# Layer 0 of a two-layer cross-attention kernel: norms placed behind the turned keys' factor, last maxima of the argmax quarters two places later, weights loaded by ScalarE's queue

## The chip, the cores and the metric

The kernel runs on one core of a Trainium2 chip. A core has five engines, each of which runs its own list of instructions in order: TensorE (PE in the profile, with its weight loads as PEld), VectorE (DVE), ScalarE (ACT), GpSimd (POOL) and SyncE (SP), which here only issues DMAs. They wait for each other through semaphores. SBUF is the on-chip memory of 128 partitions; TensorE writes its products to the banks of PSUM, from which VectorE or ScalarE fetch them. The metric is device time in microseconds, the median of several executions. The kernel before takes 1864.41 us (median of 3 runs, 1863.96 to 1866.86).

## What is computed

32 sequences of 64 tokens of width 512 pass through two layers, each a cross-attention and a feed-forward part, always added to x. The change touches layer 0's attention and the choice that prepares its feed-forward part. Cut to these:

```python
x = x + L0_xattn(layernorm(x), ctx)
def L0_xattn(text, features):
    features_n = rmsnorm(features, fn_w)
    Q = rmsnorm(text @ Wq.T + bq, qn_w)
    K = rmsnorm(features_n @ Wk.T + bk, kn_w)
    attn = softmax(Q @ K.T * D ** -0.5)
    return attn @ features_n
x = x + L0_ffn(layernorm(x))
def L0_ffn(x):
    inter = x @ c1_w.T @ c2_w.T               # 1792 wide
    idx = argmax of each block of 32 in inter # 56 choices a token
    h = relu(w1[idx] . x);  return sum of h * w2t[idx]
...                                           # layer 1: 32-head attention, clustered feed-forward
```

All of it is float32.

## The kernel before

**Tiles and pairs.** The 2048 tokens are 16 tiles of 128 rows, worked on as NP = 8 pairs of two tiles (index tt or u). Layer 0's attention is one loop over i from 0 to 7, at whose step i pair i is projected and the scores of pair i - 1 and the values of pair i - 2 are done. This text calls step i "iteration i".

**The chain of one pair.** `norm(i)` takes the tokens' mean and variance (`ln_stats`, L104 and L105), the root of the variance on ScalarE (L330), a reciprocal (L331) and then writes the normed tokens `xn` (`ln_apply`, L108, two instructions). `norm_context` squares and sums the context on ScalarE (L341), takes the root (L342) and a reciprocal (L343): `rs`, the context's factor. `keys_of` turns `xn` (transposes on TensorE at the helper's line L181, a copy on ScalarE at L365), multiplies the turned context `ct` with WK (`pk`, L372), and evacuates with factor and bias to `kb` (L375). `queries_of` multiplies the turned tokens with WQ (`pq`, L392), adds the bias (`qb`, L393), and turns that (`ptq`, copied by L400). In the next iteration `turn_keys` multiplies `kb` with its norm (L410), turns it (`ptk`) and writes the turned keys times a column of weights, `kT` (L415, two instructions). `scores` multiplies queries and `kT` (`psc`, L427), takes the maximum (L432), scales it (L434), takes exponentials on ScalarE (L440), and writes the weighted context, `cn` times `rs` times `fnb`, in place (L446, two instructions), which the values need. An iteration later `turn_scores` (L454, L456) and `add_values` (`po`, L466) make the values, and L472 adds them to x.

**The argmax.** A tile has four quarters of 448 columns (14 blocks of 32). `two_quarters(p, v)` computes two of them for pair p (`pi`, L277, into PSUM), and `first_largest` takes block maxima (`m`, L267), compares (`e`, L268, `is_equal`), lets GpSimd multiply `e` with a falling ramp (L272), and hands back a function for the last instruction, the maximum of that product (`choice`, L273). These functions wait in the list `begun`; `choose_begun` empties it at the start of the next `two_quarters`. The table PLAN says at which iteration and which of three places (0 to 2) these steps stand: `two_quarters` for pair 0 at (4,1), (4,2), (5,0), (5,1), for pair 1 at (6,0), (6,1), (7,0) and once behind the loop; `turn_choice`, which empties the list too, at (5,2).

**What sets the order.** The kernel's text gives a program order; a scheduler builds each engine's list from it, the earlier instruction of the program first, but one that it reckons ready sooner may overtake. `tc.issue_after(ins)` places what its block adds behind `ins` in the list of the same engine (an order, no wait). `started_behind(normed)` makes GpSimd's weight sums of an iteration (for w2, and eight of w1 in iterations 3 to 7, L127) wait until the weighted context of that iteration is written.

**Buffers.** The products `pk`, `pq`, `po` and `pi` share three PSUM banks (`ps_m`, tag `pm`), taken in turn. `e0`, the tile of `e`, has two buffers, the default of its pool; `xn` two, `cn` four.

**Loads.** SyncE issues all DMAs. At the start: four parts of the first context `ct` with four parts of WK between them, the tokens of pair 0, four parts of WQ, the context of pair 0, two biases, the tokens of pair 1, and so on (L476 to L488). WK is multiplied by a column on VectorE (L491) before its first use.

Of the kernel before, what the change touches and what calls it, by code (L numbers as in the profile page):

```python
# [8 lines left out]
F32 = mybir.dt.float32  # L9
# [3 lines left out]
ALU = mybir.AluOpType  # L13
# [3 lines left out]
P = 128  # L17
# [3 lines left out]
C = D // P  # L21
NT = B * S // P
INTER = 1792
QW = 448
# [11 lines left out]
def tile_kernel(  # L36
# [25 lines left out]
    nc = tc.nc  # L62
# [39 lines left out]
    def ln_stats(mv, t):  # L102
        st = small.tile([P, 6], F32, name="st", tag="st")
        nc.vector.bn_stats(st, X[t])  # L104
        nc.vector.bn_aggr(mv, st)  # L105

    def ln_apply(xn, t, mean, rstd):
        nc.vector.tensor_scalar(xn, X[t], mean, rstd, ALU.subtract, ALU.mult)  # L108
# [75 lines left out]
    with ExitStack() as l0:  # L184
# [106 lines left out]
        with ExitStack() as pa:  # L291
            wpool = pa.enter_context(tc.tile_pool(name="l0w", bufs=1))
            wk = pa.enter_context(tc.tile_pool(name="l0work", bufs=2))
# [32 lines left out]
            def norm_tokens(i, rs):  # L326
                mv = small.tile([P, 2, 2], F32, name="mv2", tag="mv2")
                for tt in range(2):
                    ln_stats(mv[:, tt, :], 2 * i + tt)
                nc.scalar.activation(rs, mv[:, :, 1], AF.Sqrt, bias=eps5)  # L330
                nc.vector.reciprocal(rs, rs)  # L331
                xn = wk.tile([P, 2, D], F32, name="xn", tag="xn")
                for tt in range(2):
                    ln_apply(xn[:, tt, :], 2 * i + tt, mv[:, tt, 0:1], rs[:, tt : tt + 1])
                return xn

            def norm_context(cn, rs):
                ss = small.tile([P, 2], F32, name="ss", tag="ss")
                for tt in range(2):
                    scr = wk.tile([P, D], F32, name="scr", tag="scr", bufs=1)  # L340
                    nc.scalar.activation(scr, cn[:, tt, :], AF.Square, accum_out=ss[:, tt : tt + 1])  # L341
                nc.scalar.activation(rs, ss, AF.Sqrt, bias=eps6, scale=1.0 / D)  # L342
                nc.vector.reciprocal(rs, rs)  # L343

            def norm(i, cn):

                rs = small.tile([P, 4], F32, name="rs4", tag="rs4")
                xn = norm_tokens(i, rs[:, 0:2])
                if i > 0:
                    norm_context(cn, rs[:, 2:4])  # L350
                return xn, rs

            def norm_of(sq):
                nc.scalar.activation(sq, sq, AF.Sqrt, bias=eps6, scale=1.0 / D)
# [52 lines left out]
            def turn_keys(kb, sq):  # L407
                kT = [wk.tile([P, C, P], F32, name="kT", tag="kT") for _ in range(2)]
                for tt in range(2):
                    nc.vector.tensor_scalar(  # L410
                        kb[:, tt, :], kb[:, tt, :], sq[:, 2 + tt : 3 + tt], None, ALU.mult
                    )
                    pt = ps_t.tile([P, C, P], F32, name="ptk", tag="pt")
                    transposed(pt, kb[:, tt, :])
                    nc.vector.tensor_mul(kT[tt], pt, wqk[:, :, None].to_broadcast([P, C, P]))  # L415
                return kT

            def scores(cn, rs, qT, sq, kT, one=None):


                psc = ps_s.tile([P, 2, S], F32, name="psc", tag="psc")
                for u in range(2):
                    for c in range(C):
                        for h in (1, 0):
                            half = slice(h * S, (h + 1) * S)
                            with tc.high_priority(offset=100) if u or c or not h else ExitStack():
                                product = nc.tensor.matmul(  # L427
                                    psc[half, u, :], qT[:, u, c, half], kT[h][:, c, u * S : (u + 1) * S],
                                    start=c == 0, stop=c == C - 1, skip_group_check=True,
                                )  # L430
                nm = small.tile([P, 2], F32, name="nm", tag="nm")
                nc.vector.tensor_reduce(nm, psc, AX.X, ALU.max, negate=True)  # L432
                if one is None:
                    most = nc.vector.tensor_mul(nm, nm, sq[:, 0:2])  # L434
                else:
                    most = nc.vector.scalar_tensor_tensor(nm, nm, one, sq[:, 0:2], ALU.mult, ALU.mult)
                s1 = wk.tile([P, 2, S], F32, name="s1", tag="s1")
                sm = small.tile([P, 2], F32, name="sm", tag="sm")
                for u in range(2):
                    nc.scalar.activation(  # L440
                        s1[:, u, :], psc[:, u, :], AF.Exp,
                        bias=nm[:, u : u + 1], scale=sq[:, u : u + 1], accum_out=sm[:, u : u + 1],
                    )

                for tt in range(2):
                    normed = nc.vector.scalar_tensor_tensor(  # L446
                        cn[:, tt, :], cn[:, tt, :], rs[:, 2 + tt : 3 + tt], fnb, ALU.mult, ALU.mult
                    )
                nc.vector.reciprocal(sm, sm)
                return s1, sm, (product.ins, most.ins, normed.ins)  # L450

# [23 lines left out]
            for c in range(C):  # L475
                nc.sync.dma_start(ct[0][:, c, :], cT[0][:, c, 0 : 2 * P])  # L476
                if c == 0:
                    nc.sync.dma_start(colt, cols)
                nc.sync.dma_start(WK[:, c, :], wk0[:, c, :])
            load_tokens(0)  # L480
            for c in range(C):
                nc.sync.dma_start(WQ[:, c, :], wq0[:, c, :])
            cn = {0: load_context(0)}
            nc.sync.dma_start(bk, bk0.to_broadcast([P, D]))
            nc.sync.dma_start(bq, bq0.to_broadcast([P, D]))
# [35 lines left out]


            steps = [prep_steps(p, ps_t) for p in range(2)]
            choices, made, begun = {}, {}, []

            def step(p, k):
                made[p] = steps[p][k]()

            def choose_begun():
                while begun:  # L530
                    begun.pop(0)()

            def two_quarters(p, v):
                choose_begun()
                if v == 0:
                    choices[p] = new_choices()
                two = []
                for q in (2 * v, 2 * v + 1):
                    pi = ps_m.tile([P, 1, D], F32, name="pi0", tag="pm")[:, :, 0:QW]

                    with tc.high_priority(offset=100) if two else ExitStack():
                        key_product(pi[:, 0], made[p][1], q // 4, q % 4)
                    two.append((q, pi))
                for q, pi in two:
                    e = wk.tile([P, QW], F32, name="e0", tag="e0")
                    c = choices[p][q // 4][:, NBQ * (q % 4) : NBQ * (q % 4) + NBQ]
                    begun.append(first_largest(pi, e, c, 1))

# [25 lines left out]
            NP = NT // 2  # L574
            store = None
            ready = norm(0, cn[0])
            keys, scored, last = {}, {}, []

            def turn_and_add(i):
# [4 lines left out]
            for i in range(NP):  # L584
# [22 lines left out]
                now = ready  # L607
                if 0 < i < NP - 1:
                    ready = norm(i + 1, cn[i + 1])
                place(i, 0)  # L610
                xn, rs = now
                kb, sq, xT = keys_of(i, ct.pop(i), xn, rs)
                if i == 0:
                    ready = norm(1, cn[1])
                if i:
                    rs1, kb1, sq1, qT = keys.pop(i - 1)
                    add = turn_and_add(i - 2) if i > 1 else lambda: None
                    kT = turn_keys(kb1, sq1)
                    add()
                    *scored[i - 1], (_, _, normed) = scores(cn[i - 1], rs1, qT, sq1, kT)  # L620
                    with started_behind(normed):
                        sum_up()
                        for n in range(*{3: (0, 2), 4: (2, 4), 5: (4, 6), 6: (6, 7), 7: (7, 8)}.get(i, (0, 0))):
                            w = [t[:, :, QW * (n // 4) : QW * (n // 4) + QW] for t in W1]
                            four_sums(nc.gpsimd, w[4:], *w[:4], False, (n % 4,))
# [18 lines left out]
            xT, choices = made[1][0], choices[1]  # L644
# [4 lines left out]
        with ExitStack() as pb:  # L649
            wk = pb.enter_context(tc.tile_pool(name="ffnwork", bufs=2, reuse_waits="tile"))  # L650
# [131 lines left out]
            for p in range(NP):  # L782
# [18 lines left out]
                if choosing:  # L801
                    choices = new_choices()
# [28 lines left out]
    with ExitStack() as pc:  # L831
# [3 lines left out]
        wk = pc.enter_context(tc.tile_pool(name="l1work", bufs=2, reuse_waits="tile"))  # L835
# [303 lines left out]
        kT = keys(kvs[0])  # L1139
        qT, qsq = project_q(xts, 0, 0)  # L1140
        last = None
        for n, (T, g) in enumerate(units):
# [21 lines left out]
            if more:  # L1164
# [5 lines left out]
                kT = keys(kvs[g2 % 2])  # L1170
# [159 lines left out]
```

## Time and profile before

| what | value |
|---|---|
| median of 3 runs | 1864.41 us (1866.86, 1863.96, 1864.41) |
| profiled execution, its own time | 1866.38 us |
| its span in the profile | 1864.6 us, 29382 instructions |
| mean granted clock of TensorE | 0.992 of full speed |
| DMA | 204.58 MB, 110 GB/s on the mean, on one hardware queue beside two of the instructions |
| layer 0's attention | from 0 to about 188 us, then `ph` (L720) of its feed-forward part begins |
| busy from 100 to 120 us | PE 18.84, DVE 14.38, ACT 9.38, POOL 12.50 us |
| busy from 120 to 140 us | PE 17.39, DVE 14.66, ACT 9.23, POOL 8.34 us, granted clock 0.83 |

A line of the profile names engine, line of the kernel, operation and tiles (out <- in). A list in order of time starts with the start and the length in us (of xN instructions together) and ends, in brackets, with the idle time of the engine before it and what ended that. A row of a table by stretches gives the stretch, its length, the busy time of PE, PEld, DVE, ACT and POOL with the number of instructions, then the granted clock of TensorE, the mean busy share of the 16 DMA engines and GB/s. The ends of TensorE's products are modelled, so that a busy PE is not one at its peak.

### The profile page before, as it was taken

How to read it: one execution, taken by the hardware profiler on the slowest of the kernel's cores; microseconds unless marked ns; L12 is line 12 of the kernel's file. 1: busy time of each engine (PE TensorE's matmuls, PEld its weight loads, DVE VectorE, ACT ScalarE, POOL GpSimd, SP SyncE). 2: the span in 40 equal slices, each digit the busy share in tenths (PEclk: the TensorE clock that was granted, in tenths of full speed). 3: DMA queues.
4: the chain of work that ended last, by engine and by line, in shares of the span. 5: the costliest groups of instructions: out<-in, count | busy, mean ns of one | idle time of the engine just before them, and what ended most of it. 6: DMA issues, size and time to landing. Idle time of an engine off the chain costs nothing.

```text
span 1864.6 us, 29382 instructions
## 1 busy us (share of the span) xinstructions
PE 1825.8 (98%) x11612; PEld 1468.1 (79%) x11612; DVE 940.8 (50%) x1715; ACT 652.1 (35%) x1183; POOL 718.8 (39%) x622
## 2 busy tenths in 40 slices
PE   8999999999999999999999999999999999999997
PEld 4544988888998888878888888888888888888753
DVE  5877555555425444345543444444434544444566
ACT  4644322222113333334333333333334333333470
POOL 1542444444336676564322343323224333242300
PEclk9999999999999999999999999999999999999998
DMA  8631400000024444444444354444443444443203
GB/s 242 184 114 53 160 22 21 21 22 21 21 68 151 131 131 149 149 163 135 142 130 131 108 151 122 118 130 119 130 145 116 119 130 119 130 119 96 80 1 90
DMA packets 153592, 204.58 MB, mean 110 GB/s; under 512 B 14512, under 2 KB 95152, under 8 KB 152816
## 3 DMA queue, kind: packets, MB, share of 16 engines
q1 hardware_dynamic: 153456, 202.72, 36.4%
q8 instruction: 92, 1.51, 0.3%
q14 instruction: 44, 0.36, 0.1%
HBM read 173.60 MB, written 29.07 MB: 109 GB/s over the span
## 4 chain that ended last, share of the span: by engine, by line
PE 85%; DVE 4%; POOL 4%; DMA 3%; ACT 3%; issue 2%; SPq 0%; POOLq 0%; ACTq 0%
PE b L893 45%; PE ph L720 10%; PE po L763 9%; PE sc L1046 3%; PE pv L1098 3%; PE pd L1231 3%; POOL prob L1053 2%; PE pr L1015 2%; PE pq L392 2%; PE pta L1083 2%; DVE x L1126 1%; PE pt L181 1%; PE pk L372 1%; DMA x<-in_x 1%; PE pi L277 1%
## 5 line engine op out<-in xcount | busy, mean ns | idle before, releaser
L893 PE MATMUL b<-tx,wq 128*128 128x256 f32 x1024 | 242.8, 381 | 0.5 <-ACT keep L901 0.5
L893 PE MATMUL b<-wo,so 128*128 128x256 f32 x1024 | 233.7, 381 | 3.9 <-DVE x L1126 2.0
L893 PEld LDWEIGHTS b<-wo,so 128*128 128x128 f32 x1024 | 193.0, 190 | 36.1 <-DVE x L1126 9.8
L893 PEld LDWEIGHTS b<-tx,wq 128*128 128x128 f32 x1024 | 191.3, 190 | 31.2 <-issue 6.0
L127 POOL TENSOR_TENSOR so<-oT 128x512 f32<-128x512 f32 x64 | 80.1, 1274 | 338.8 <-ACT oT L1104 338.6
L1126 DVE TENSOR_TENSOR x<-x,b 128x512 f32<-128x512 f32 x224 | 153.4, 685 | 93.3 <-PE b L893 91.7
L893 PE MATMUL b<-wo,oT 128*128 128x256 f32 x768 | 190.0, 383 | 0.0
L893 PE MATMUL b<-xt,wq 128*128 128x256 f32 x768 | 186.9, 381 | 0.0
L901 ACT COPY keep<-b 128x512 f32<-128x512 f32 x144 | 84.1, 585 | 266.1 <-PE b L893 266.1
L893 PEld LDWEIGHTS b<-wo,oT 128*128 128x128 f32 x768 | 143.0, 190 | 20.1
L893 PEld LDWEIGHTS b<-xt,wq 128*128 128x128 f32 x768 | 141.8, 190 | 21.1 <-issue 4.0
L1053 POOL TENSOR_TENSOR prob<-prob,msk 128x512 f32<-128x512 f32 x64 | 80.1, 1273 | 198.8 <-DVE prob L1052 198.8
L982 DVE TENSOR_TENSOR qT<-b,keep 128x512 f32<-128x512 f32 x96 | 66.3, 691 | 129.1 <-PE b L893 129.1
L984 ACT ACTIVATE qsq<-qT 128x512 f32<-128x512 f32 x128 | 80.9, 632 | 116.4 <-DVE qT L982 115.4
L893 PE MATMUL b<-wkv,sc 128*128 128x256 f32 x512 | 115.7, 379 | 0.0
L272 POOL TENSOR_TENSOR e<-e,down 128x896 f32<-128x896 f32 (+1 forms) x40 | 68.3, 1713 | 102.3 <-DVE e L268 92.5
L893 PEld LDWEIGHTS b<-wkv,sc 128*128 128x128 f32 x512 | 97.3, 190 | 13.2
L763 PE MATMUL po<-w,gT 128*128 128x256 f32 x448 | 101.9, 382 | 0.0
L763 PEld LDWEIGHTS po<-w,gT 128*128 128x128 f32 x448 | 84.0, 190 | 18.7 <-issue 7.8
L1061 ACT ACTIVATE prob<-prob 128x512 f32<-128x512 f32 x64 | 40.5, 632 | 150.5 <-POOL prob L1058 150.5
L953 DVE TENSOR_TENSOR kv<-b,keep 128x512 f32<-128x512 f32 x48 | 33.2, 691 | 116.5 <-PE b L893 116.5
L893 PE MATMUL b<-wkv,ct 128*128 128x256 f32 x384 | 91.4, 379 | 0.0
(197 smaller groups left out, 3133.2 us busy)
## 6 DMA issues: line engine op xcount, KB each, us to landing
wq<-in_wq SPq DMA_DIRECT2D x104, 256.0 KB
wo<-in_wo SPq DMA_DIRECT2D x104, 256.0 KB
wq<-wqs SPq DMA_DIRECT2D x96, 256.0 KB
wo<-wos SPq DMA_DIRECT2D x96, 256.0 KB
wkv<-in_wkv SPq DMA_DIRECT2D x52, 256.0 KB
wkv<-wks SPq DMA_DIRECT2D x48, 256.0 KB
wqs<-wq SPq DMA_DIRECT2D x32, 256.0 KB
wos<-wo SPq DMA_DIRECT2D x32, 256.0 KB
```

Of the source, the lines that this page charges most:

```text
L127: ins = eng.tensor_tensor(s[k], *pairs[k], op)
L272: nc.gpsimd.tensor_tensor(e3, e3, down[:, None, :].to_broadcast([P, k, BLK]), ALU.mult)
L720: nc.tensor.matmul(ps[:, c, :], W1[LEFT[i]][:, d, (c0 + c) * P : (c0 + c + 1) * P], xq[RIGHT[i]][:, d, :], start=first and c == 0 and d == ...
L763: nc.tensor.matmul(ps, chunk(gq[LEFT[i]], c), W2[RIGHT[i]][:, c, :], start=first and c == 0, stop=c == HC - 1, skip_group_check=True,)
L893: last = nc.tensor.matmul(out[:, h, :], lhs(h, c), rhs(h, c), start=first and h == 0 and c == 0, stop=c == 1, skip_group_check=True,)
L901: nc.scalar.copy(e, ps)
L982: nc.vector.tensor_add(o, ps, kept.rearrange("p j (b t) -> p j b t", t=S))
L984: nc.scalar.activation(qsq[:, 4 * th : 4 * th + 4, 2 * hh : 2 * hh + 2, :], o, AF.Square)
L1046: nc.tensor.matmul(sc[k * S : (k + 1) * S, 4 * a + 2 * pp + b, :], qT[:, at, 2 * pp + k, :], kT[:, bb * S : (bb + 1) * S], start=True, sto ...
L1053: nc.gpsimd.tensor_tensor(pr, pr, msk_b, ALU.add)
L1098: one = nc.tensor.matmul(pv[b][:, a, :], kv[rows, 2 * h + a, HD : 2 * HD], aTs[h][rows, a, :], start=True, stop=True,).ins
L1126: added.append(nc.vector.tensor_add(xq[:, i, j], xq[:, i, j], ps).ins)
```

## The change

Four things, in the order of the diff. `norm_tokens` no longer writes `xn` itself but hands back `apply`, which does. The call before the loop and iteration 0 run it at once, as before; iterations 1 to 6 run it after `add()`, inside `issue_after(kT_done[-1])`, where `kT_done` is a new list of the last `kT` instruction of each `turn_keys`. The two instructions of the weighted context in `scores` are put into such a block as well. `two_quarters` leaves the last two entries of `begun` in the list, and `e0` has four buffers. The four loads each of WK and WQ are issued by ScalarE.

```diff
                 xn = wk.tile([P, 2, D], F32, name="xn", tag="xn")
-                for tt in range(2):
-                    ln_apply(xn[:, tt, :], 2 * i + tt, mv[:, tt, 0:1], rs[:, tt : tt + 1])
-                return xn
+
+                def apply():
+                    for tt in range(2):
+                        ln_apply(xn[:, tt, :], 2 * i + tt, mv[:, tt, 0:1], rs[:, tt : tt + 1])
+
+                return xn, apply
...
-                    nc.vector.tensor_mul(kT[tt], pt, wqk[:, :, None].to_broadcast([P, C, P]))
+                    done = nc.vector.tensor_mul(kT[tt], pt, wqk[:, :, None].to_broadcast([P, C, P]))
+                kT_done.append(done.ins)
                 return kT
...
                 for tt in range(2):
-                    normed = nc.vector.scalar_tensor_tensor(
-                        cn[:, tt, :], cn[:, tt, :], rs[:, 2 + tt : 3 + tt], fnb, ALU.mult, ALU.mult
-                    )
+                    with tc.issue_after(kT_done[-1]):
+                        normed = nc.vector.scalar_tensor_tensor(
+                            cn[:, tt, :], cn[:, tt, :], rs[:, 2 + tt : 3 + tt], fnb, ALU.mult, ALU.mult
+                        )
...
-                nc.sync.dma_start(WK[:, c, :], wk0[:, c, :])
+                nc.scalar.dma_start(WK[:, c, :], wk0[:, c, :])
             load_tokens(0)
             for c in range(C):
-                nc.sync.dma_start(WQ[:, c, :], wq0[:, c, :])
+                nc.scalar.dma_start(WQ[:, c, :], wq0[:, c, :])
...
-            def choose_begun():
-                while begun:
+            def choose_begun(left=0):
+                while len(begun) > left:
                     begun.pop(0)()

             def two_quarters(p, v):
-                choose_begun()
+                choose_begun(2)
...
-                    e = wk.tile([P, QW], F32, name="e0", tag="e0")
+                    e = wk.tile([P, QW], F32, name="e0", tag="e0", bufs=4)
...
                     kT = turn_keys(kb1, sq1)
                     add()
+
+                    if i < NP - 1:
+                        with tc.issue_after(kT_done[-1]):
+                            ready[2]()
                     *scored[i - 1], (_, _, normed) = scores(cn[i - 1], rs1, qT, sq1, kT)
```

More of the change, by code (lines that the diff above doesn't have):

```diff
@@ L347, in norm @@
                 rs = small.tile([P, 4], F32, name="rs4", tag="rs4")
-                xn = norm_tokens(i, rs[:, 0:2])
+                xn, apply = norm_tokens(i, rs[:, 0:2])
                 if i > 0:
                     norm_context(cn, rs[:, 2:4])
-                return xn, rs
+                return xn, rs, apply
             def norm_of(sq):
@@ L523, in tile_kernel @@
             steps = [prep_steps(p, ps_t) for p in range(2)]
-            choices, made, begun = {}, {}, []
+            choices, made, begun, kT_done = {}, {}, [], []
             def step(p, k):
                 made[p] = steps[p][k]()
-            def choose_begun():
-                while begun:
+            def choose_begun(left=0):
+                while len(begun) > left:
                     begun.pop(0)()
             def two_quarters(p, v):
-                choose_begun()
+                choose_begun(2)
                 if v == 0:
@@ L610, in tile_kernel @@
                 place(i, 0)
-                xn, rs = now
+                xn, rs, _ = now
                 kb, sq, xT = keys_of(i, ct.pop(i), xn, rs)
@@ L614, in tile_kernel @@
                     ready = norm(1, cn[1])
+                    ready[2]()
                 if i:
@@ L619, in tile_kernel @@
                     add()
+                    if i < NP - 1:
+                        with tc.issue_after(kT_done[-1]):
+                            ready[2]()
                     *scored[i - 1], (_, _, normed) = scores(cn[i - 1], rs1, qT, sq1, kT)
```

## The prediction

> **What bounds the kernel now.** I read the page first. TensorE (PE) is busy 98% of the span, so a microsecond counts only if PE stands still in it or runs at a lower clock.
>
> ```profile
> PE 1825.8 (98%) x11612; PEld 1468.1 (79%) x11612; DVE 940.8 (50%) x1715; ACT 652.1 (35%) x1183; POOL 718.8 (39%) x622
> ```
>
> The change touches layer 0's attention only, 0 to about 188 us. Next I asked whom PE waits for in the first 300 us:
>
> ```profile
> PE pk L372 <- DVE WK L491: 5.5, 1, 5.5
> PE psc L427 <- DVE kT L415: 3.3, 3, 2.1
> PE pk L372 <- DVE e L268: 1.2, 1, 1.2
> ```
>
> The columns are total, times, longest. One wait of 2.1 us, of the scores for the turned keys kT, and one of 1.2 us, of the keys' product for an argmax comparison e (`is_equal`), stand out behind the head's 5.5 us. Both lie in iteration 5. The granted clock was read by stretches of 2 us there (third figure from the end):
>
> ```profile
> 120.00:122.00 2.00, 1.01 (x8) 0.13 (x8) 2.00 (x4) 0.05 (x1) 0.73 (x1) 1.00 0.79 242
> 122.00:124.00 2.00, 0.89 (x16) 0.89 (x18) 2.00 (x4) 0.68 (x2) 1.35 (x1) 0.78 0.71 133
> 124.00:126.00 2.00, 2.00 (x26) 1.40 (x22) 1.24 (x4) 0.00 (x0) 0.00 (x0) 0.50 0.96 344
> 126.00:128.00 2.00, 2.00 (x7) 1.01 (x4) 1.17 (x5) 1.83 (x4) 0.00 (x0) 0.50 0.20 68
> 128.00:130.00 2.00, 2.00 (x4) 0.83 (x3) 1.29 (x5) 1.89 (x4) 1.26 (x2) 0.52 0.46 103
> 130.00:132.00 2.00, 2.00 (x6) 0.88 (x5) 1.52 (x3) 0.00 (x0) 1.43 (x2) 1.00 0.41 159
> ```
>
> PE idles, then runs at half clock: 2.0 us x (0.22 + 0.50 + 0.50 + 0.48) = 3.4 us lost. VectorE's (DVE) list in order of time tells why PE idled:
>
> ```profile
> 117.68 0.62 DVE L273 TENSOR_REDUCE choice<-e 128x14 f32<-128x448 f32 x1 [0.50 <-POOL e L272]
> 118.22 0.74 DVE L375 SCALAR_TENSOR_TENSOR kb<-pk,rs,bk 128x512 f32<-128x512 f32 x1
> 118.88 1.00 DVE L108 TENSOR_SCALAR xn<-x,mv,rs 128x512 f32<-128x512 f32 x2
> 119.79 1.41 DVE L446 SCALAR_TENSOR_TENSOR cn<-cn,rs,fnb 128x512 f32<-128x512 f32 x2
> 121.11 0.75 DVE L375 SCALAR_TENSOR_TENSOR kb<-pk,rs,bk 128x512 f32<-128x512 f32 x1
> 121.77 1.28 DVE L415 TENSOR_TENSOR kT<-ptk,wqk 128x512 f32<-128x512 f32 x2
> ```
>
> Four norm instructions (2.4 us) and last maxima that wait for GpSimd (POOL) stand before kT, and DVE runs its list in order.
>
> **Layer norm and context weighting behind kT.** Nothing is added or removed: two `xn` (about 0.5 us each), two `cn` (0.72) per pair move from before kT to after it; no DMA moves. In iteration 5 the keys' last product ends about 118.9, so without the four, kb could end near 119.7 and kT, 1.28 us behind it, near 121.0, just when PE ends the values before the scores; iterations 3, 4, 6 and 7, where kT follows kb directly, have no wait of the scores at all. So the 2.10 us go. In iteration 2 a `cn` pair slowed to 2.84 us by POOL holds kb back, and the scores wait 0.52: 0.5 us go. In iteration 1 the scores wait 0.64 and a transpose 0.40; but kT there also stands behind the context factor's reciprocal (L343, at 36.10), which waits for ScalarE and the context's DMA at 34.26 and is not moved. Between 0 (the DMA holds it) and 1.0 I take 0.6.
>
> What it costs is behind kT. A product in the argmax needs one of three PSUM banks, and the second query product gets the bank of the first argmax quarter, once e has read it. In iteration 6:
>
> ```profile
> 148.63 1.41 DVE L472 SCALAR_TENSOR_TENSOR x<-po,sm,x 128x512 f32<-128x512 f32 x2
> 150.81 1.15 DVE L267 TENSOR_REDUCE m<-pi 128x14 f32<-128x448 f32 x2
> 151.88 1.15 DVE L268 TENSOR_TENSOR e<-pi,m 128x448 f32<-128x448 f32 x2
> ...
> 150.65 7.13 PE L392 MATMUL pq<-WQ,xT 128*128 128x512 f32 x16
> ```
>
> kT ends at 148.57; e is done with the first quarter at 152.5 (3.9 us later) and PE comes to the second query product at about 154.2 (5.6 later). Put xn (1.0) and cn (1.44) in between and e is done 6.4 us after kT: PE waits 0.8. In iterations 4 and 5 PE has four transposes or the summed product more to do (about 0.5 us), so 0.3 each. Cost 1.4 us. Below nothing it can't go; above, 3 x 2.9 us if POOL slows the four (third rival). POOL's weight sums start behind `cn` and so also move later: the cn of pair 2 now runs at 38.6 though its scores come at 74.6, and the sums of iterations 3 to 7 were carried forward with it. They now land beside the argmax of iterations 4 to 6; the last would end near 175, ahead of FFN products that begin at 187.9: 0.
>
> **The clock.** The Trainium skill ("TensorE: Matmul & The Clock Gate", on HAM oscillation) gives as its rule no PE gaps over about 3.4 us, as the gate judges free-running windows of that length. By it, a gap of 2.10 us costs 2.10 and its removal brings no clock. The rows say otherwise: the gap, with 1.2 us of PE work ahead of it in the same window, was followed by 6.8 us at half clock. I take the row: 3.4 us go with the gap (by the rule, 0). It needs no idle left in that window near 2 us; the residue above is 0.3. A second half-clock stretch, around 185 to 191 at the end of the stage, comes from a serial tail (scores, exponentials, turn, values) that isn't changed; where the windows fall in it moves with everything before, up or down by half a window's clock: 0, plus or minus 1.7 us.
>
> **Last maximum two places later, four buffers for e.** The 14 maxima stay; DVE's waits for POOL before them (7.6 us in all) lose most of their weight because the next quarters' comparisons, which free PSUM, now come first. At 110.63 a maximum waits 1.52 us for POOL, itself behind sums whose DMA was late, and comparison and the keys' bank stand behind it: the 1.16 us at 111.83 go. Between 0 (the order keeps the maximum early, as only its place in the program moves) and 1.16 I take 1.16. The final argmax, with an empty list before it, is as before.
>
> **Weights by ScalarE's queue.** Eight issues of 0.43 to 0.56 us leave SyncE (SP); ScalarE does them where it has a table load and then nothing until 14.29. SP reaches the tokens 4 x 0.47 = 1.9 us earlier. Is that worth 1.9 us? The DMA share (next to last figure):
>
> ```profile
> 2.00:4.00 2.00, 0.00 (x0) 0.00 (x0) 0.33 (x2) 0.01 (x1) 1.33 (x8) 1.00 0.70 199
> 4.00:6.00 2.00, 0.48 (x1) 0.48 (x2) 0.49 (x1) 0.00 (x0) 0.00 (x0) 1.00 0.96 275
> 8.00:10.00 2.00, 2.00 (x4) 0.62 (x2) 0.49 (x1) 0.00 (x0) 0.00 (x0) 1.00 0.99 267
> ```
>
> The skill's "DMA: Bandwidth & Descriptors" (section on issuing engines, and its table of advice) says that spreading transfers over issuing engines doesn't help bandwidth, as all use the same 16 engines and interleave; only issue time is saved. The trace agrees that the engines are full from 4 us on, so what can be gained is the 30% of 2 to 4 us: 0.6 us, not 1.9. Interleaving cuts both ways: the query weights, 1 MB not needed until 16.8, now share with the first tokens, which may land up to about 0.6 us later than 12.7. But both ways meet again at the second pair's tokens (landing 22.4, behind the same 4 MB in either order), for which PE waits 0.89 at 26.14 through DVE. I take 0.6 faster there (ends: 0.6 slower, 1.0 faster).
>
> **Sum**, against the profiled execution's own 1866.4 us (span 1864.6): head -0.6, iteration 1 -0.6, iteration 2 -0.5, bank -1.16, kT -2.10, clock -3.4, argmax banks +1.4 = -7.0, so 1859.4. From 186 to 520 us PE waits 0.4 us in all, so the gain is passed on whole. The median of the three runs is 1864.4, 2.0 below the profiled one, and the runs lie in two groups (1864.0 and 1864.4; 1866.9): a size that fits a part of a clock window, so the 3.4 us may be smaller in the median run. Without any of it: 1864.4 - 3.6 = 1860.8; with all, 1857.4. 1859.4 lies between, and I keep it.
>
> **Rivals.**
> 1. Forecast, 0.53: 1859.4, own range 1856 to 1862.
> 2. Part of it is not there, 0.22: either the maxima stay early in DVE's list and the 1.16 us remains (1860.6), or the half clock is a matter of the profiled execution's window and the median run only gets the stalls (1860.8). For it: the two groups of runs, and that no ordering edge holds the maxima back. Against: the waits' cause, a maximum ahead of a comparison, is turned around in program order. It ends at 1860 to 1864.
> 3. Slower, 0.12: what is moved behind kT takes the place of the stall. If POOL shares those stretches, xn takes 1.0 (as at 87.4 us, 0.94) and cn 1.42 each (as at 50.4 us): 4.84 us, e is done 8.8 after kT, and PE waits 2.7 to 3.2 in each of iterations 4, 5 and 6, 8.8 in all; one of these gaps trips the clock again. 1866.4 - 8.4 + 8.8 + 3.4 = 1870.2. It decides from about 3.5 us of work in between, where the stall exceeds 1.5. Against: POOL is idle from 93.0 to 100.2 and from 117.7 to 121.3 and starts only behind cn.
> 4. More, 0.13: the end's windows fall well and iteration 1 gives its full 1.0: 1859.4 - 1.7 - 0.4 - 0.5, some 1856.5.
>
> A measurement of this kernel can tell about 0.2% (3.7 us) from no change, so faster means under 1860.7. Of case 1 some 0.40 lies there, of 2 0.05, of 4 all: 0.58. Slower: 0.12. The rest, 0.30, is the same. The range reaches from 1854.5 to 1866.5, leaving out most of case 3 and the ends.
>
> **What would show it.** In the changed profile kT follows kb directly in every iteration and no wait of psc for kT is over 0.5 us; the granted clock is 1.00 from 100 to 175 us; pk no longer waits for e; L446 of a pair comes after its L415; POOL's 896-wide sums reach to about 170. Right at the cost: small waits of pq for L268 in iterations 4 to 6. The page's DMA part has a second queue and a bk, bq and cn landing at about the same times. I am wrong if pq waits over 1.5 us for L268 or L472, if half-clock stretches stay two or grow, or if the head's first transpose comes over 1 us later than 15.5.

## The result, and the profile after

| | median, us | runs | profiled execution: span, mean clock |
|---|---|---|---|
| before | 1863.96 (1862.82 to 1866.86) | 9 | 1864.6, 0.992 |
| after | 1870.82 (1863.95 to 1877.22) | 9 | 1862.2, 0.996 |

The ratio is 1.0039, with a 95% interval of 1.0025 to 1.0052: about 7 us slower. The profiled execution of after took 1863.95 us, the least of its nine, so its stretches say what happens in it, and the runs say what it costs. Even there the changed stage ends later: the first product `ph` of the feed-forward part starts at 190.51 us, against 187.86 before (190.54 in a second profile of the changed kernel, h1). The rest, in which nothing was changed, then took 5.0 us less, in an execution with a mean clock of 0.996 against 0.992.

The page's row of busy time of after:

```profile
PE 1822.5 (98%) x11612; PEld 1466.2 (79%) x11612; DVE 935.8 (50%) x1715; ACT 651.1 (35%) x1183; POOL 717.9 (39%) x622
```

Three rows of the view of waits of after, between 12 and 190 us (who waited for what, total, times, longest):

```profile
PE ptq L181 <- DVE qb L397: 6.6, 7, 1.5
PE pt L181 <- DVE xn L108: 1.8, 1, 1.8
PE pq L396 <- DVE kb L379: 0.9, 1, 0.9
```

The work is the same. The waits for kT (3.3 us) and of pk for `e` (1.2) are gone; in their place PE waits for `qb`, the queries with their bias, seven times, 6.6 us against 0.9 before, and in the head for the first tokens. Six of the seven, 6.2 us, lie in iterations 4 to 6, where PE never waits for `qb` before (its 0.9 us are at 26 us). VectorE's list in order of time shows the cause:

```profile
95.84 0.99 DVE L108 TENSOR_SCALAR xn<-x,mv,rs 128x512 f32<-128x512 f32 x2
...
99.00 0.74 DVE L452 SCALAR_TENSOR_TENSOR cn<-cn,rs,fnb 128x512 f32<-128x512 f32 x1
...
105.06 0.62 DVE L273 TENSOR_REDUCE choice<-e 128x14 f32<-128x448 f32 x1 [3.01 <-POOL e L272]
105.59 0.68 DVE L104 BATCH_NORM_STATS2 st<-x 128x6 f32<-128x512 f32 x1
106.19 0.67 DVE L397 TENSOR_TENSOR qb<-pq,bq 128x512 f32<-128x512 f32 x1
...
122.78 0.75 DVE L379 SCALAR_TENSOR_TENSOR kb<-pk,rs,bk 128x512 f32<-128x512 f32 x1 [2.68 <-PE pk L376]
123.44 1.28 DVE L419 TENSOR_TENSOR kT<-ptk,wqk 128x512 f32<-128x512 f32 x2
...
159.47 0.62 DVE L273 TENSOR_REDUCE choice<-e 128x14 f32<-128x448 f32 x1 [3.75 <-POOL e L272]
160.00 0.68 DVE L397 TENSOR_TENSOR qb<-pq,bq 128x512 f32<-128x512 f32 x1
```

kT follows kb directly, as intended (122.78, 123.44). But a last maximum (L273) stands ahead of `qb` and waits 3.01 us for GpSimd, and again 3.75 in iteration 6 (and 3.12 in iteration 5). VectorE runs its list in order, so a `qb` whose product is ready waits behind it. Before, at the place of the first, the maximum waited 0.39 us, and GpSimd stood idle until `e` came (two lines of VectorE, one of GpSimd):

```profile
101.38 0.62 DVE L273 TENSOR_REDUCE choice<-e 128x14 f32<-128x448 f32 x1 [0.39 <-POOL e L272]
103.68 0.67 DVE L393 TENSOR_TENSOR qb<-pq,bq 128x512 f32<-128x512 f32 x1
100.21 2.23 POOL L272 TENSOR_TENSOR e<-e,down 128x448 f32<-128x448 f32 x2 [7.22 <-DVE e L268]
```

GpSimd's list of after at the first place says why it was late:

```profile
99.82 2.08 POOL L127 TENSOR_TENSOR w<-w,w 128x896 f32<-128x896 f32 x1 [10.49 <-DVE cn L452]
101.86 2.07 POOL L127 TENSOR_TENSOR w1s<-w,w1s 128x896 f32<-128x896 f32 x1
103.89 1.13 POOL L272 TENSOR_TENSOR e<-e,down 128x448 f32<-128x448 f32 x1
```

And TensorE's list of after says what that cost:

```profile
106.92 0.66 PE L181 MATMUL ptq<-ident,qb 128*128 128x128 f32 x4 [0.90 <-DVE qb L397]
109.57 1.11 PE L181 MATMUL ptq<-ident,qb 128*128 128x128 f32 x4 [1.04 <-DVE qb L397]
...
160.74 0.66 PE L181 MATMUL ptq<-ident,qb 128*128 128x128 f32 x4 [1.46 <-DVE qb L397]
```

GpSimd had been idle for 10.49 us waiting for `cn`, then ran two weight sums of 2.08 us, and only then the ramp product of an `e` that had been ready since 101.3. Before, the eight sums of w1 started between 46 and 121 us; held behind the later `cn`, they start from 79.8 to 175.6, those from 99.8, 128.6 and 154.2 on beside the argmax of iterations 4 to 6. (In iteration 6 it is one sum of w1 with four short ones of w2 around it, 0.72 us each, that stand ahead of the ramp.) The two gaps of about 1 us lie 2.7 us apart, and the table by stretches of after (granted clock third from the end) shows what follows them:

```profile
106.00:108.00 2.00, 1.10 (x9) 0.72 (x8) 2.00 (x6) 0.98 (x3) 1.92 (x3) 1.00 0.00 1
108.00:110.00 2.00, 0.96 (x6) 0.43 (x3) 1.64 (x6) 1.16 (x3) 1.92 (x4) 0.85 0.02 4
110.00:112.00 2.00, 2.00 (x14) 0.86 (x14) 1.97 (x5) 1.97 (x7) 2.00 (x3) 0.50 0.00 0
112.00:114.00 2.00, 2.00 (x7) 0.71 (x6) 1.63 (x4) 0.82 (x4) 1.97 (x3) 0.50 0.00 0
114.00:116.00 2.00, 2.00 (x8) 1.52 (x7) 2.00 (x5) 1.16 (x2) 1.01 (x2) 0.50 0.02 4
```

PE works half of 106 to 110, then runs at half clock to 116. That the gaps bring the half clock on is not shown (last section).

### The profile page after: what moved, and what is told of

Read it like the earlier page. It is cut to its first block, busy times and chain, and to the rows that moved or that the text cites. A ratio compares the mean times of both kernels' runs of the same rounds, so it can differ in the third digit from the quotient of the medians.

```text
span 1862.2 us, 29374 instructions
## 1 busy us (share of the span) xinstructions
PE 1822.5 (98%) x11612; PEld 1466.2 (79%) x11612; DVE 935.8 (50%) x1715; ACT 651.1 (35%) x1183; POOL 717.9 (39%) x622
## 4 chain that ended last, share of the span: by engine, by line
PE 89%; DVE 5%; POOL 3%; issue 1%; DMA 1%; ACT 1%; SPq 0%; ACTq 0%; POOLq 0%; DVEq 0%
PE b L905 48%; PE ph L732 10%; PE po L775 9%; PE sc L1058 3%; PE pv L1110 3%; PE pd L1243 3%; PE pk L376 2%; PE pr L1027 2%; POOL prob L1065 2%; PE pta L1095 2%; PE pq L396 1%; PE pt L181 1%; DVE x L1138 1%; PE ptk L1015 1%; PE pi L277 1%
## 5 line engine op out<-in xcount | busy, mean ns | idle before, releaser
L775 PE MATMUL po<-w,gT 128*128 128x256 f32 x448 | 101.9, 382 | 0.0
```

The source lines that it names most:

```text
L775: nc.tensor.matmul(ps, chunk(gq[LEFT[i]], c), W2[RIGHT[i]][:, c, :], start=first and c == 0, stop=c == HC - 1, skip_group_check=True,)
```

## The experiments

Theory G: GpSimd's sums, pushed back by `cn` into the argmax, delay ramp, maximum and `qb`. Rivals: R, the moved norms cost by themselves (VectorE's room, the banks behind kT); Q, the second queue costs. The edit of each kernel is named by the parts it has: X is xn behind kT, C is cn behind kT, M is the maxima two places later with four buffers, W is the second queue; E is an added ordering edge. Each ratio is to the kernel before on the same chip (its medians 1861.8 to 1864.7 over 235 runs). It is not the quotient of the two medians: that is 1.0013 for g2 and 1.0011 for i2. The last column is PE's wait for qb in the profiled execution, from 12 to 190 us. It does not order the kernels by itself: e4 and g3 have about the same wait.

| kernel | parts | runs | ratio (95%) | us (times) |
|---|---|---|---|---|
| h1_after_again | X C M W | 9 | 1.0039 (1.0026 to 1.0052) | 6.6 (7) |
| e3_queue_back | X C M | 6 | 1.0040 (1.0025 to 1.0054) | 7.0 (8) |
| i1_queue_back_again | X C M | 21 | 1.0028 (1.0019 to 1.0037) | 6.7 (7) |
| e1_cn_free | X M W | 21 | 1.0017 (1.0009 to 1.0025) | 3.1 (2) |
| e4_xn_back | C M W | 11 | 1.0032 (1.0021 to 1.0043) | 2.8 (2) |
| g1_sums_free | X C M W, sums free | 14 | 1.0000 (0.9988 to 1.0012) | 2.5 (2) |
| h3_xn_max | X M | 13 | 1.0001 (0.9993 to 1.0009) | 3.5 (3) |
| i2_cn_max | C M | 13 | 1.0003 (0.9994 to 1.0013) | 2.8 (2) |
| g2_cn_alone | C | 22 | 1.0005 (0.9995 to 1.0015) | 3.0 (3) |
| h4_xn_alone | X | 13 | 1.0001 (0.9991 to 1.0010) | 1.6 (2) |
| g3_max_alone | M | 20 | 0.9994 (0.9984 to 1.0004) | 3.1 (2) |
| f4_queue_alone | W | 22 | 1.0016 (1.0008 to 1.0025) | 0.2 (1) |
| e2_hold_max | X C M W E | 22 | 1.0015 (1.0007 to 1.0024) | 2.0 (2) |
| f1_hold_queue | X C M E | 22 | 0.9985 (0.9974 to 0.9996) | 3.2 (3) |
| f2_hold_cn_queue | X M E | 18 | 0.9984 (0.9975 to 0.9992) | 1.1 (1) |
| f3_hold_alone | M E | 6 | 0.9955 (0.9940 to 0.9970) | 0.5 (1) |
| h2_hold_again | M E | 7 | 0.9982 (0.9969 to 0.9996) | none |
| g4_edge_alone | E | 22 | 0.9985 (0.9976 to 0.9993) | 0.7 (1) |

**The sums.** First one part at a time was taken back, cn (e1_cn_free) and xn (e4_xn_back):

```diff
-                    with tc.issue_after(kT_done[-1]):
-                        normed = nc.vector.scalar_tensor_tensor(
+                    normed = nc.vector.scalar_tensor_tensor(
...
```

> The changed kernel, with the weighted context (cn) free to stand before kT again; xn, maxima and queue stay as changed. Theory G (GpSimd): cn behind kT pushes GpSimd's weight sums, which start behind cn, ahead of the ramp products of e; the last maximum waits for those on VectorE (3.0 to 3.8 us in iterations 4 to 6) and qb stands behind it. Freed, the sums of w1 end before 125 us, the maxima wait under 1 us, PE's waits for qb fall from 6.6 us to under 2, and the median is 4 to 8 us under the changed kernel's 1870.8, at or under the kernel before (1864.0). Theory R (room): it is the work itself, xn and cn in the room behind kT, that delays e and qb; freeing cn (1.4 of 2.4 us) brings about half of the 6.6 us, some 3 us. Theory Q (queue): no change, 1870.

```diff
+                    ready[2]()
...
-                    if i < NP - 1:
-                        with tc.issue_after(kT_done[-1]):
-                            ready[2]()
```

> The changed kernel with xn of the next pair written at once again, not behind kT. Theory G: the cause stands (cn behind kT), the maxima still wait about 3 us for GpSimd, PE waits over 5 us for qb: median 1868 to 1872. Theory R: 1.0 of the 2.4 us behind kT is gone, so about 2 to 3 us of PE's waits for qb and banks go: 1867 to 1868.

cn free takes off 0.22% and more than half of the waits for qb; xn free takes off 0.07%, within the intervals. Neither decides between G and R. In e1 the waits fell to 3.1 us, not under 2, and the kernel stayed 0.17% over the one before; in e4 they fell to 2.8, where G had said over 5, and the median, 1867.5, is in R's range. The direct trial leaves cn and xn where the change put them and frees only the eight sums of w1:

```diff
                     with started_behind(normed):
                         sum_up()
+                    if True:
                         for n in range(*{3: (0, 2), 4: (2, 4), 5: (4, 6), 6: (6, 7), 7: (7, 8)}.get(i, (0, 0))):
```

> The changed kernel, but GpSimd's eight weight sums of w1 (896 wide) no longer start behind cn; cn and xn stay behind kT and the weights on the second queue. Theory G (the sums, pushed back by cn into the argmax, delay the ramp products, the maxima and so qb): the sums run early again, no maximum waits over 1 us for GpSimd before a qb, TensorE's waits for qb fall from 6.6 us to under 3, and the time is as with cn free, 1.000 to 1.002 of the kernel before. Rival R (the moved xn and cn themselves cost, by room on VectorE and the argmax banks): waits for qb stay over 5 us and the time stays at 1.003 to 1.005.

It measured 1.0000, the lower end of what theory G named; R's 1.003 to 1.005 is out. One sign was missed: in iteration 6 a maximum still waits 1.84 us, behind the sums of w2, which this kernel leaves behind cn. That g1, which keeps the second queue, lies below e1 and below that queue's own 1.0016 (f4), is at the edge of the intervals and has no explanation here. GpSimd's list of g1_sums_free at the same argmax:

```profile
106.75 1.13 POOL L272 TENSOR_TENSOR e<-e,down 128x448 f32<-128x448 f32 x1 [15.90 <-DVE e L268]
```

And VectorE's:

```profile
107.92 0.62 DVE L273 TENSOR_REDUCE choice<-e 128x14 f32<-128x448 f32 x1 [0.53 <-POOL e L272]
```

GpSimd now waits for `e`, not `e` for it, and the maximum waits 0.53 us instead of 3.01.

**Parts alone and in pairs.** The kernel before with single parts put in:

> The kernel before with one part of the change: cn behind kT. Theory G: the sums start behind it and so run beside the argmax of iterations 4 to 6; maxima wait 3 us each for GpSimd ahead of qb, TensorE waits over 5 us for qb, and the kernel is 3 to 6 us slower than before (1.0015 to 1.003), although the 2.10 us wait for kT in iteration 5 is shorter. Rival Q (only the second queue costs): 0 to 5 us faster than before (0.997 to 1.000).

Missed: 1.0005, not 1.0015 to 1.003. The wait for qb came, but 3.0 us of it, not over 5, and kT's wait shrank from 3.3 to 1.1. So cn alone is not the whole loss. It need not be free: the quotient of its medians is 1.0013, and at one granted clock it is slower than before (last section).

> The kernel before with xn behind kT alone. The prediction's own terms for xn: a part of the 2.10 us at kT and of its half clock gone (up to 5 us), some 0.6 us for the banks: 0.998 to 1.000. Rival R: it costs in every one of six iterations by the bank of the values and of the argmax, 1.001 to 1.002.

> The changed kernel without two of its parts: cn stays where it was, and the weights stay on the first queue, so xn behind kT and the later maxima are left. Theory G with the queue: no sums beside the argmax and no late tokens, hence no slower than before, 0.998 to 1.000. Rival R (xn behind kT holds the argmax banks up and costs by itself): 1.001 to 1.003.

> The kernel before with cn behind kT and the later maxima, without xn and without the second queue. Theory G: this is the pair that costs, sums late and maxima behind them: 1.0015 to 1.0025 of before, though cn alone has 1.0005 and the maxima alone 0.9994. Rival: it takes xn behind kT as well (three parts together), and the pair is at 0.999 to 1.0005.

xn alone and xn with the later maxima make no difference in time, as theory G said and R did not. Their mean clock, though, is 0.9952 and 0.9951 against 0.9941 of the kernel before beside them, so some cost of the moved xn may be hidden behind a higher clock. i2_cn_max missed theory G's 1.0015 to 1.0025 and met its rival: cn and the maxima need xn beside them for the loss (i1_queue_back_again, 1.0028, on the same chip). Why, two pairs of lists show. VectorE's of i2_cn_max (cn behind kT, xn not):

```profile
94.21 1.40 DVE L452 SCALAR_TENSOR_TENSOR cn<-cn,rs,fnb 128x512 f32<-128x512 f32 x2
95.53 1.40 DVE L478 SCALAR_TENSOR_TENSOR x<-po,sm,x 128x512 f32<-128x512 f32 x2
...
98.25 1.14 DVE L268 TENSOR_TENSOR e<-pi,m 128x448 f32<-128x448 f32 x2
100.93 0.62 DVE L273 TENSOR_REDUCE choice<-e 128x14 f32<-128x448 f32 x1 [1.55 <-POOL e L272]
```

GpSimd's of the same kernel:

```profile
97.73 2.08 POOL L127 TENSOR_TENSOR w1s<-w,w1s 128x896 f32<-128x896 f32 x1
99.77 2.23 POOL L272 TENSOR_TENSOR e<-e,down 128x448 f32<-128x448 f32 x2
```

VectorE's of i1_queue_back_again (xn, cn and maxima):

```profile
93.81 0.99 DVE L108 TENSOR_SCALAR xn<-x,mv,rs 128x512 f32<-128x512 f32 x2
94.72 1.40 DVE L478 SCALAR_TENSOR_TENSOR x<-po,sm,x 128x512 f32<-128x512 f32 x2
...
96.97 0.74 DVE L452 SCALAR_TENSOR_TENSOR cn<-cn,rs,fnb 128x512 f32<-128x512 f32 x1
...
98.70 0.61 DVE L268 TENSOR_TENSOR e<-pi,m 128x448 f32<-128x448 f32 x1
...
103.04 0.62 DVE L273 TENSOR_REDUCE choice<-e 128x14 f32<-128x448 f32 x1 [3.01 <-POOL e L272]
```

GpSimd's of that kernel:

```profile
99.83 2.08 POOL L127 TENSOR_TENSOR w1s<-w,w1s 128x896 f32<-128x896 f32 x1
101.87 1.13 POOL L272 TENSOR_TENSOR e<-e,down 128x448 f32<-128x448 f32 x1
```

Without xn, cn follows kT at once, and the sums are nearly done when `e` comes. With xn behind kT, cn falls behind xn and the values' sum `x`, the sums end 2.1 us later (101.9 against 99.8), and so does the ramp, while `e` comes at the same time. The maximum then ends at 103.7 instead of 101.6, and the qb behind it are late. The pair xn and cn without the later maxima was not run, so it is not shown that the maxima are needed too.

**The maxima.** The scheduler put the maxima of the first quarters of iterations 4, 5 and 6 straight behind their `e` (in the changed kernel's list `e` at 101.45, the maximum next), although the program has them two places later. An edge holds each maximum behind the latest qb:

```diff
-                    nc.vector.tensor_add(qb[:, tt, :], pq, bq)
+                    qb_done.append(nc.vector.tensor_add(qb[:, tt, :], pq, bq).ins)
...
-                    begun.pop(0)()
+                    with tc.issue_after(qb_done[-1]):
+                        begun.pop(0)()
```

It was put into the changed kernel (e2), into that without the queue (f1) and also without cn (f2), and into the kernel before with the later maxima (f3, twice) and without them (g4); g3 has the later maxima and no edge.

> The changed kernel, with every last maximum that is taken from the list placed by an order edge behind the latest qb. Theory G: GpSimd's sums stay late and its ramp products too, but nothing waits for them in front of qb, so PE's waits for qb fall from 6.6 us to under 2 and the median falls by 4 to 8 us, to 1863 to 1867. Theory R: xn and cn still stand in front of e, so the products in the argmax still take 1.5 instead of 1.0 us and qb stays late; the median stays over 1868. Theory Q: no change, 1870.

> The changed kernel with the maxima held behind qb and the weights on SyncE's queue; xn and cn stay behind kT. Theory G with Q2: what remains is the intended change alone; 1.5 to 2.5 us under the run with only the maxima held (1863.7), so 1861 to 1862, level with the kernel before or just under it. Theory R (room behind kT): banks and qb still late, no better than 1863.

> The changed kernel with the maxima held behind qb, the weights on SyncE's queue and cn free to stand before kT; only xn stays behind kT. Theory G: GpSimd's sums come early and nothing waits for it: the fastest so far, 1857 to 1860. Theory R: with 1.0 instead of 2.4 us behind kT the pi products take about 1.0 us each again; also 1857 to 1860. If it is over 1862, neither names the cause of what is left.

> The kernel before, with only the maxima two places later, four buffers for e, and the maxima placed by an edge behind the latest qb; xn, cn and queue as before. Theory G: no sums are late, the keys' wait of 1.2 us for e goes, the scores' wait of 2.1 us for kT in iteration 5 shrinks since the maxima no longer hold up kb; 2 to 5 us faster than the kernel before, 1857 to 1860. Rival: kT stays behind xn and cn in iteration 5, the clock falls as before, and no more than 1.2 us are gained.

> The kernel before with places, buffers and edge of the maxima, the version of the six runs at 0.9955. If place and edge complete each other (each alone 0.9994 and 0.9985): 0.995 to 0.9965. If those six runs had luck with the clock: 0.997 to 0.9985, as the edge alone.

> The kernel before with the maxima two places later in the program and four buffers for e, and no ordering edge. If the place in the program is what counts (as the prediction took it), the wait of pk for e (1.16 us) and most of kT's 2.10 go, and the time is that of the version with the edge (0.9955, about 8 us less than before). If the edge is what counts, since the scheduler puts a maximum straight behind its e anyway, the gain is under half of that: 0.998 to 1.000.

> The kernel before with only the ordering edge that holds a maximum behind the latest qb; the list is emptied as before and e has two buffers. If the edge is what counts: as with edge and two places, 0.995 to 0.997 of before. If the places are needed too (a maximum held behind qb is still ahead of the next comparisons): 0.998 to 1.000, and a wait of pk or pi for e stays.

e2 went as theory G said (1863.7 us, in its 1863 to 1867; R had over 1868): 0.24% below the changed kernel, which leaves 0.15%, what the second queue costs alone. With the edge cn's place no longer matters: f1 and f2 differ by 0.0001, although f1's cn is as late as ever. f1 met its 1861 to 1862, f2 missed its 1857 to 1860 by 0.9 us. The places alone bring nothing that can be told (0.06%). The edge alone brings 0.15%, less than the 0.3 to 0.5% it was given if it were all that counts, though no wait of pk or pi for `e` stayed. f3's 0.9955 did not hold: its six runs had a mean clock of 0.9963 against 0.9936 of the kernel before beside them; the second time, at 0.9941 for both, it is 0.9982. Whether places and edge together beat the edge alone stays open. VectorE's list of h2_hold_again:

```profile
97.68 1.14 DVE L268 TENSOR_TENSOR e<-pi,m 128x448 f32<-128x448 f32 x2
...
100.58 0.69 DVE L397 TENSOR_TENSOR qb<-pq,bq 128x512 f32<-128x512 f32 x1 [0.56 <-PE pq L396]
...
104.01 0.69 DVE L397 TENSOR_TENSOR qb<-pq,bq 128x512 f32<-128x512 f32 x1 [2.60 <-PE pq L396]
104.62 1.14 DVE L273 TENSOR_REDUCE choice<-e 128x14 f32<-128x448 f32 x2
```

Both qb come first and wait for TensorE alone; both maxima run behind them without a wait. This is what the prediction thought the places would do.

**The second queue.**

```diff
-                nc.scalar.dma_start(WK[:, c, :], wk0[:, c, :])
+                nc.sync.dma_start(WK[:, c, :], wk0[:, c, :])
...
-                nc.scalar.dma_start(WQ[:, c, :], wq0[:, c, :])
+                nc.sync.dma_start(WQ[:, c, :], wq0[:, c, :])
```

so for e3 and i1; f4 is the reverse in the kernel before.

> The changed kernel with WK and WQ issued by SyncE again. Theories G and R: the first transposes come at 15.5 us again instead of 16.8, but PE comes to the first scores at 37.5 in both, so the median changes by less than 1.5 us and stays near 1870. Theory Q: the kernel is 3 us or more faster, near 1866.

> The changed kernel with the weights back on the first queue (xn, cn, maxima as changed), again, since six runs gave 1.0040. If the queue costs the 0.16% that it costs alone and parts add: 1.0039 - 0.0016, so 1.002 to 1.0025. If the queue's cost is hidden by the later waits for qb: 1.0035 to 1.004.

> The kernel before, with only WK and WQ moved to ScalarE's queue. Theory Q2 (from the four runs so far: with ScalarE's queue the first scores of pair 0 came at 37.5 to 39.3 us, with SyncE's at 36.1): the query weights share the DMA engines with the first tokens and contexts, the first transposes come 1 to 2 us later and the kernel is 1 to 2.5 us slower than the kernel before (1863 to 1865 beside 1862). Rival (the step as predicted): 0.6 us faster, or nothing, as both orders meet again at the second pair's tokens.

Alone it costs 0.16%, 3.0 us, a little over the 1 to 2.5 of theory Q2. Five pairs differ by it: f4 and before 0.0016, e1 and h3 0.0016, e2 and f1 0.0030, e4 and i2 0.0029, h1 and i1 0.0011; four of them across chips. e3's six runs showed nothing of it, the twenty-one of i1 do, at 1.0028 a little over the 1.002 to 1.0025 of the theory that parts add. VectorE's list in the head of f4_queue_alone:

```profile
15.31 1.29 DVE L104 BATCH_NORM_STATS2 st<-x 128x6 f32<-128x512 f32 x2 [3.66 <-DMA x<-in_x]
```

TensorE's there:

```profile
18.07 1.07 PE L181 MATMUL pt<-ident,xn 128*128 128x128 f32 x8 [1.81 <-DVE xn L108]
```

The first tokens' statistics start at 15.3 us (14.1 in after, 12.75 in before, 12.8 in i1): between 14.1 and 15.3 in all seven kernels with the second queue, between 12.3 and 13.3 in the others. Two things are seen. WQ's loads are now issued beside the tokens, from 4.9 us in after instead of 6.4, so that they share the engines; that this is what delays the tokens is argued, not shown. And the tokens are hardly issued earlier, for SyncE waits for the first `ct` to land. Its line and its row of waits (0 to 20 us) in after, and its line before:

```profile
4.35 2.65 SPq L312 DMA_DIRECT2D x<-in_x  x2
SPq L312 <- DMA ct<-in_cT: 2.5, 2, 1.3
4.97 1.40 SPq L312 DMA_DIRECT2D x<-in_x  x2
```

In f4 it is 5.17.

**The changed kernel again.**

> The changed kernel again, on the chip of the three beside it. If the 0.4% of the first nine runs is the change's own: 1.0025 to 1.005 of before. If it was a matter of few runs with much half clock: 1.001 to 1.0025. Theory G with the queue (parts of about 3 us for the queue and 4 for the late qb) expects 1.003 to 1.004.

The same 1.0039 in nine further runs: the size is the change's own.

## Why the prediction was wrong

It said 1859.4 us, with faster the likeliest sign. Point by point:

- **kT, the keys' bank, iteration 2** (-2.10, -1.16, -0.5): as worked out. No psc waits for kT, and pk no longer for `e`, in the changed kernel's profile. The waits went; that the time went with them no run shows apart, and xn with the later maxima, which lacks these waits too (h3), is no faster than before. **Argmax banks** (+1.4): about as sized, by luck; not as a wait of pq for `e`, of which there is none, but in the group of four `pi` ahead of it, which takes 1.50 us in iterations 4, 5 and 6 against 1.02 in 4 and 6 before (5 ran at half clock then): 3 x 0.48 = 1.4.
- **The failed step is the weight sums**: "They now land beside the argmax of iterations 4 to 6; the last would end near 175, ahead of FFN products that begin at 187.9: 0." The place and the time are right (175.6 + 2.1), the 0 is not. It asked whether the sums' own readers would wait, and not who stands behind them on GpSimd: the ramp products, and behind these the maxima and qb. That is 6.6 - 0.9 = 5.7 us of PE waits. Three ways of ending it give time back: the sums of w1 freed (g1) 0.39%, the maxima held behind qb (e2) 0.24%, cn freed (e1) 0.22%. With the second queue's own 0.16% the last two make up the whole; g1 overshoots, unexplained, as said above.
- **The step that would have covered it** was the maxima: their waits "lose most of their weight because the next quarters' comparisons, which free PSUM, now come first". The scheduler kept the maxima of the (4,1), (5,1) and (6,1) quarters straight behind `e`; held behind qb by an edge, they do what was meant (h2). The second rival had named this ("the maxima stay early in DVE's list"), but priced it at 1.16 us, as if the waits stayed as they were; with the sums in front they grew, in iteration 6 from 1.53 to 3.75.
- **Head** (-0.6): the sign was wrong. SyncE came to the tokens 0.6 us earlier, not 1.9, and they landed later: f4 measures +3.0 (h1 against i1 +2). The prediction's slow end, 0.6, was too near: the tokens came 1.3 us late, and PE then waited again for the context's factor (0.91). Its own sign came true: the head's first transpose starts at 16.82, over 1 us after 15.5.
- **The clock** (-3.4): taken from one execution with a low clock. Its mean is 0.992; of the 235 runs of the kernel before, 21 had 0.992 or less, and their mean was 0.9938. At some 1.9 us per thousandth (last section) that execution lost about 3 us more than the mean one; where in it, no trace tells, so it stays open how much of the 3.4 us the usual execution has, and whether the gap brought the half clock on (last section). The text said so as a doubt and kept the figure. Some of it may have come: with xn behind kT and no late sums the clock is higher by about 0.001 (h3, h4). But in the changed kernel it is 0.9931 in the mean of 18 runs, and without the second queue 0.9925 and 0.9927 (e3, i1).
- **The third rival**, at 1870.2, had the size but not the way: it moved slower norms in front of the comparisons, with PE waiting for pq's bank. No pq waited so, and xn and cn were not slowed (0.99 us for two, 0.74 for one).

Added up afterwards, against the median of before: -0.6 - 0.5 - 1.16 - 2.1 + 1.4 = -3.0 for the parts taken to have held, +5.7 for qb, +2 to +3 for the queue and 0.0007 x 1864 = 1.3 for the clock make +6.0 to +7.0; measured is 0.0039 x 1864 = +7.3. The first five of these terms were not timed apart, and waits in one profiled execution are not microseconds of the median, so this sum shows that the parts are of the right size and no more.

## What to carry to other kernels

When an instruction moves later, follow everything that starts behind it on other engines, and ask for each who is queued behind it there; work with slack of its own can still stand in front of work without any. A later place in the program doesn't hold an instruction back where a scheduler builds the lists: read where it ended up, and use an ordering edge if it must stand behind something. Before a loss seen in one profiled execution is counted as a gain, compare that execution's clock with those of the other runs.

## What the runs showed of the hardware

- A kernel's run time follows its mean clock: for the 235 runs of the kernel before, the medians are 1867.05 us at 0.992 (18 runs), 1864.51 at 0.993 (86), 1862.63 at 0.994 (69), 1861.12 at 0.995 (36) and 1857.54 at 0.997 (7), about 1.9 us per thousandth on the whole. So two kernels can be compared at one clock on one chip as well, and the moved norms then show a price that the ratios hide. At 0.994 cn alone is at 1866.57 us (6 runs) and the kernel before beside it at 1863.64 (18), 2.9 less; at 0.995 xn with the later maxima is at 1862.49 (7) against 1860.74 (4). The queue alone, at 0.993, is at 1867.89 (11) against 1865.70 (26). The clock is itself a result of what a kernel does, so this parts the cost in two and does not replace the ratio.
- Half clock came without a gap that a rule names, and what brings it stays open. The Trainium skill ("TensorE: Matmul & The Clock Gate", HAM oscillation) warns of idle gaps over about 3.4 us; in the changed kernel's layer 0 none is over 1.8 behind the head's first wait. Two of about 1 us, 2.7 us apart, stand ahead of its six microseconds near half clock, and the same place slows in h1 (0.54 and 0.60 in 112 to 116) and for longer in i1, with the same gaps. But it slows as well where the view of waits has none of PE from 96 to 118 us, as in h2, g4 and e2. The table by stretches of h2:

```profile
106.00:108.00 2.00, 2.00 (x12) 0.79 (x10) 1.94 (x5) 2.00 (x7) 2.00 (x4) 0.97 0.00 0
108.00:110.00 2.00, 2.00 (x6) 0.74 (x5) 1.34 (x4) 0.14 (x1) 2.00 (x2) 0.50 0.00 0
110.00:112.00 2.00, 2.00 (x7) 1.48 (x6) 2.00 (x4) 1.17 (x2) 1.54 (x3) 0.50 0.03 8
112.00:114.00 2.00, 2.00 (x3) 0.67 (x2) 2.00 (x4) 0.00 (x0) 1.00 (x1) 0.50 0.00 0
```

  PE is busy all of 98 to 118 us there and is at half clock from 108 to 114. Before, with a gap of 1.16 us at the same place, the clock stays at 1.00. So such gaps are not needed for it, and the list of PE's waits alone does not foretell the clock.
- The same skill says in "DMA: Bandwidth & Descriptors" (Issuing engines are not separate DMA queues) that issuing from several engines only saves issue time. Here even that was small, 0.6 us at the tokens, and the whole was not neutral but 3.0 us slower; the likely reason, not isolated, is that WQ's 1 MB, not yet needed, came to share the engines with 0.5 MB of tokens that were.
